# Layer norms of a recurrent kernel: eleven backward items normalised as they lie, by turned and spread mean and scale, instead of turned to tokens and back

## The chip, the cores and the metric

The kernel runs on one core of a Trainium2 chip. Its time is the device time of one execution in microseconds; runs of the same kernel are compared by their median. The engines are named as in the profile: PE (TensorE matmuls) and PEld (its weight loads), DVE (VectorE), ACT (ScalarE), POOL (GpSimd) and SP (SyncE, which here only issues DMAs). Each engine works through its own instructions in program order and waits for others by semaphores.

## The reference, cut to what matters

Input x is 8 sequences of 512 tokens with 512 features, all float32. A bidirectional recurrent stack of four layers works on the normalised x, forward and on the flipped sequence; then a linear fusion and a feed-forward part with ternary weights follow, each with a residual.

```python
def _mingru(x, Wz, bz, Wh, bh):
    z = jax.nn.sigmoid(jnp.einsum('bsi,hi->bsh', x, Wz) + bz)
    h_tilde = jnp.tanh(jnp.einsum('bsi,hi->bsh', x, Wh) + bh)
    a = jnp.clip(1.0 - z, CLAMP_LO, CLAMP_HI)
    return _linear_scan(a, z * h_tilde)          # h[t] = a[t] * h[t-1] + z[t] * h_tilde[t]

def _stack(x, Wz, bz, Wh, bh, gamma, beta):
    h = x
    for i in range(L):                           # L = 4
        h_new = _mingru(h, Wz[i], bz[i], Wh[i], bh[i])
        if i > 0:
            h_new = h_new + h
        h = _layernorm(h_new, gamma, beta)       # over the features
    return h
...
h_fwd = _stack(x, ...)
h_bwd = jnp.flip(_stack(jnp.flip(x, axis=1), ...), axis=1)
out = concat(h_fwd, h_bwd) @ fusion_W.T + fusion_b
```

Both matrices of a layer are the same weights and both directions use the same ones, so one product u per layer and item gives z, h_tilde and a. The scan runs along the tokens; the norm needs mean and variance over the features of each token.

## The kernel before

**Layout.** A state is held transposed: features on the 128 partitions in NC_ = 4 chunks, the 512 tokens along the free dimension, so that a scan is one DVE instruction per chunk. For the norm that is the wrong way round: mean and variance belong to a token, that is to a column. So `norm` turns the result: `turned` transposes the four chunks of 128 tokens into one PSUM tile `pt` (tokens on partitions, L316), `stats` takes mean and variance there (bn_stats L171, bn_aggr L173, small DVE operations L177 and L182, a power on POOL L178), `normalise` writes the normalised tokens `tok` on ACT (L188, L189), and `back` transposes them back into `pf` (L325), from where ACT writes the next layer's state with gamma and beta as per-partition scale and bias (L331).

**Items, layers, pairs.** An item is one sequence b in one direction: s = (b, 0) forward or (b, 1) backward. Sequences go in pairs (0,1), (2,3), (4,5), (6,7), called pairs 1 to 4. Layer 0 of a pair is computed in `first_layer`, interleaved with the fusion of the pair before. Layers 1 to 3 go through the items of a pair in turn, (b,0), (b,1), (b+1,0), (b+1,1), so that an item's next layer begins 16 slots after its last one did.

**Slots.** `layer` makes one `slot` for each of the 4 output chunks. A slot issues 16/4 = 4 matmuls of the gate (each two instructions in the trace, L487), the three activations a, t, z that read it (L505 to L507), the clamp of a on POOL (L511), then shares of work queued by earlier items, then on DVE the product (L514), the scan (L518) and the residual add (L588) of this gate. Two queues hold the shares: `turns` (one turn with its statistics) and `backs` (one turn back). `shares` takes the head of each queue once it is due by the slot counter `now`, and a second one only if that is late; the part that a share leaves for ACT (`last`) is issued at the slot's end. `stages` holds work due at a later slot; its kind "late" is issued right after the gate's activations. `x_shares` adds work for the next pair's x: in layers 1 and 2 of pairs 2 and 3, statistics of one tile `xn` every fourth slot. With T the first slot of an item's layer, its turns are due in slots T+5 to T+8, its backs in T+9 to T+12. `need` makes slots without a gate if an item's queued work isn't done when its next layer begins.

**Buffers.** PSUM: `ps_u` 4 (gates), `ps_t` 2 (turns), `ps_f` 2 (backs). SBUF: `z` 16, `tok` 10, states `h` 6, `t` 2 and `a` 3 per gate.

**DMA.** SP's queue is written in program order: x tiles for the next pair, the next transposed x (L105), x tiles for the fusion (`xf`, L96), in pair 4 the ternary weights and `xy`; each waits on its buffer in that order.

After the recurrent part (the first two thirds of the time) the feed-forward part follows, which the diff doesn't touch.

Of the kernel before, what the change touches and what calls it, by code (L numbers as in the profile page):

```python
# [9 lines left out]
F32 = mybir.dt.float32  # L10
F32R = mybir.dt.float32r
AF = mybir.ActivationFunctionType
ALU = mybir.AluOpType
# [3 lines left out]
P = 128  # L17
LN_EPS = 1e-5
# [6 lines left out]
def kernel(  # L25
# [26 lines left out]
    nc = tc.nc  # L52
    B, S, H = x.shape
    L = gru_wT.shape[0]
    F = fc_wT.shape[1]
    NC_ = H // P
    NT = S // P
# [7 lines left out]
    small = ctx.enter_context(tc.tile_pool(name="small", bufs=8))  # L65
    wpool = ctx.enter_context(tc.tile_pool(name="wts", bufs=1))
    hp = ctx.enter_context(tc.tile_pool(name="h", bufs=6))
    dram = ctx.enter_context(tc.tile_pool(name="x1", bufs=1, space=bass.MemoryType.DRAM))

    tokp = ctx.enter_context(tc.tile_pool(name="tok", bufs=TOK))  # L70
    xsp = ctx.enter_context(tc.tile_pool(name="xs", bufs=12))
    zp = ctx.enter_context(tc.tile_pool(name="z", bufs=ZT))
    ps_f = ctx.enter_context(tc.tile_pool(name="ps_f", bufs=2, space=PSUM))
# [34 lines left out]
    gam = const.tile([P, NC_], F32, name="gam")  # L108
    bet = const.tile([P, NC_], F32, name="bet")
# [11 lines left out]
    for i in range(2):  # L121
# [3 lines left out]
        s = fusp.tile([P, P], F32R, name=f"fpick{i}")  # L125
# [36 lines left out]
    ident = const.tile([P, P], F32, name="ident")  # L162
    make_identity(nc, ident)
    mhalf = const.tile([P, 1], F32, name="mhalf")
# [64 lines left out]
    with rec:  # L229
# [7 lines left out]
        now = [0]  # L237
        state = {}
        rsv = {}
        turns, backs = [], []  # L240

        held = [0]

        class Tokens(list):
# [4 lines left out]
            def append(self, tile_):  # L249
                super().append(tile_)  # L250
                self.at = now[0] + self.lag

        def ready(at):
            if isinstance(at, Tokens):
                return len(at) == NT and at.at <= now[0]
            return at <= now[0] and held[0] < TOK

        def shares(cap):


            last = []
            for q in (turns, backs):
                some = []
                for i in range(max(2, cap)):
                    if not q or not ready(q[0][0]):
                        break
                    at, piece = q[0][:2]
                    late = (at.at if isinstance(at, Tokens) else at) + piece <= now[0]
                    if i >= cap and not late:
                        break  # L270
                    some.append(take(q))
                last = some + last
            return last

        zlive = [0]

        left = {}

        def queue(q, key, at, piece, go):
            left[key] = left.get(key, 0) + 1  # L280
            q.append((at, piece, key, go))

        def take(q):
            _, _, key, go = q.pop(0)
            left[key] -= 1
            return go()

        def need(*keys):

            while any(left.get(k) for k in keys):  # L290
                slot(None, 2)

        def tokens(source, tok, rs, name):

            def go():
                src = source()
                found = stats(src, name, rs, tok is not None)
                if tok is None:
                    return lambda: None
                held[0] += 1  # L300

                def last():
                    tile_ = tokp.tile([P, H], F32, tag="tok", name=f"tok_{name}")
                    normalise(tile_, src, found, name)
                    tok.append(tile_)
                return last
            return go

        def turned(zs, t, name, frees=0):
            def source():  # L310
                if t == NT - 1:
                    zlive[0] -= frees
                spare = name.startswith("00_0") and t > 1
                pt = (ps_f if spare else ps_t).tile([P, H], F32, tag="pf" if spare else "pt", name=f"pt_{name}")
                for c in range(NC_):
                    nc.tensor.transpose(pt[:, ts(c, P)], zs[c][:, ts(t, P)], ident)  # L316
                return pt
            return source

        def back(toks, dst, c, affine, name):  # L320

            def go():
                pf = ps_f.tile([P, S], F32, tag="pf", name=f"pf_{name}")
                for t in range(NT):
                    nc.tensor.transpose(pf[:, ts(t, P)], toks[t][:, ts(c, P)], ident)  # L325
                if c == NC_ - 1:
                    held[0] -= NT

                def last():
                    if affine:  # L330
                        nc.scalar.activation(  # L331
                            dst()[:, c, :], pf, AF.Identity,
                            bias=bet[:, c : c + 1], scale=gam[:, c : c + 1],
                        )
                    else:
                        nc.scalar.copy(dst()[:, c, :], pf)
                return last
            return go

        def norm(s, zs, tag, pause, pair=1):  # L340

            toks, at = Tokens(), now[0] + pause

            def dst():
                if s not in state:
                    state[s] = hp.tile([P, NC_, S], F32, tag="h", name=f"h_{s[0]}{s[1]}")
                return state[s]

            for t in range(NT):
                queue(turns, s, at, t // pair, tokens(turned(zs, t, f"{tag}_{t}", NC_), toks, None, f"{tag}_{t}"))  # L350
            for c in range(NC_):
                queue(backs, s, toks, c // pair, back(toks, dst, c, True, f"{tag}_{c}"))

        def norm_last(s, tag):
            rsv[s] = small.tile([P, NT], F32, tag="rsv", name=f"rsv_{tag}")
            zs = [state[s][:, c, :] for c in range(NC_)]
            for t in range(NT):
                source, name = turned(zs, t, f"{tag}_{t}"), f"{tag}_{t}"
                queue(turns, s, now[0] + NC_ + 1, t, by_scalar(s, t, source, name) if s[0] > 1 and s[0] % 2 and s[1] == 0 else
                      tokens(source, None, rsv[s][:, t : t + 1], name))  # L360
# [17 lines left out]
        rx, scale = {}, {}  # L378
# [64 lines left out]
        def x_shares():  # L443
            return [take(q) for q in (xturns, xbacks) if q and ready(q[0][0])]
# [3 lines left out]
        stages = []  # L448
# [15 lines left out]
        def slot(work=None, cap=1, long=False):  # L464

            end = work() if work is not None else None
            due("factors")
            due("late")
            due("clamps")
            if long:  # L470
                due("scans")
            last = shares(cap) + x_shares()
            due("scans")
            if end is not None:
                end()
            due("resid")
            for f in last:
                if f is not None:
                    f()
            now[0] += 1  # L480
# [35 lines left out]
        def scan(dst, a, z, backward):  # L516
            d = slice(None, None, -1) if backward else slice(None)
            nc.vector.tensor_tensor_scan(dst[:, d], a[:, d], z[:, d], 0.0, ALU.mult, ALU.add)  # L518
# [58 lines left out]
        def layer(s, l):  # L577
            while s not in state:
                slot(None, 2)
            need(s)  # L580
            zs = []
            h = state[s]
            for o in range(NC_):
                def scans(a, z, o=o):
                    scan(z, a, z, s[1] == 1)
                    zs.append(z)
                    if l < L - 1:
                        nc.vector.tensor_tensor(z, z, h[:, o, :], ALU.add)  # L588
                    elif o == NC_ - 1:

                        for c in range(NC_):
                            def sums(c=c):
                                zlive[0] -= 1
                                nc.vector.tensor_tensor(h[:, c, :], zs[c], h[:, c, :], ALU.add)
                            stages.append((now[0] + c, "resid", sums))
                slot(gates(h, l, o, f"{s[0]}{s[1]}_{l}_{o}", scans))

                if s[0] < 2 and (l == L - 1 or o % 2) and len(extra) > 2 * NW or s == (B - 1, 1) and l == L - 1:
                    pieces(1)
            now[0] -= 1  # L600
            if l < L - 1:
                norm(s, zs, f"{s[0]}{s[1]}_{l}", 2)
            else:
                norm_last(s, f"{s[0]}{s[1]}_{l}")
            now[0] += 1
# [265 lines left out]
    for i in range(2):  # L871
# [5 lines left out]
        s = const.tile([P, P], F32R, name=f"pick{i}")  # L877
# [137 lines left out]
    for j in range(ends):  # L1015
        b, k = divmod(j, NF)
        late = []
# [22 lines left out]
        at = 12 if b == 0 else 8  # L1040
# [57 lines left out]
```

## Time and profile before

| | |
|---|---|
| time, median of 3 runs | 1712.66 us (1712.62 to 1712.66) |
| the profiled execution | 1712.95 us, of which its span 1711.2 us |
| layers 1, 2 of pair 2 | 357.90 to 427.45, 427.45 to 496.40 us |
| layers 1, 2 of pair 3 | 655.64 to 725.20, 725.20 to 794.14 us |
| layers 1, 2 of pair 4 | 953.38 to 1022.94, 1022.94 to 1091.89 us |
| granted TensorE clock | 1.00 |
| DMA | 53 GB/s over the span |

How to read it: the span runs from the first to the last instruction. A group's line gives line, engine, operation, what it writes from what, and its count, then busy time, the mean duration of one, and the idle time of the engine before it with what ended that. Durations of successive instructions of an engine overlap somewhat, so the distance from start to start is the better cost of a sequence. A matmul row that merges several instructions gives the time from the first one's start to the last one's end.

### The profile page before, as it was taken

The numbers are of one execution on the slowest core, as the hardware profiler recorded it, in microseconds if no ns is written. First come the engines' busy times: TensorE is split into PE (matmuls) and PEld (weight loads), VectorE is DVE, ScalarE is ACT, GpSimd is POOL, SyncE is SP. The second block draws the span as 40 slices with busy tenths as digits, with TensorE's granted clock in tenths as the row PEclk, the third lists the DMA queues.
The fourth block names the chain that finished last, engine by engine and source line by source line (L and its number), as shares of the span: only waits on it lengthen the run. The fifth ranks groups of instructions, "written<-read, shape, count | busy, mean of one in ns | idle before, by whom it ended". The sixth has DMA issues, their size and how long they took to land.

```text
span 1711.2 us, 19776 instructions
## 1 busy us (share of the span) xinstructions
PE 1700.3 (99%) x6440; PEld 1042.6 (61%) x6440; DVE 1389.1 (81%) x2619; ACT 1089.5 (64%) x1918; POOL 377.2 (22%) x558
## 2 busy tenths in 40 slices
PE   9999999999999999999999999999999999999999
PEld 5455554555555455555545555554688888888887
DVE  7988889889887888888788888885568768768877
ACT  5898873468886346888535688862356566666654
POOL 3333333223332222333222222321000000000000
PEclk9999999999999999999999999999999999999999
DMA  7002231150000125000012200102201101100100
GB/s 271 19 25 81 98 93 37 66 193 19 13 1 1 56 68 191 19 13 1 1 56 75 98 28 22 75 1 99 74 1 50 50 1 50 50 21 30 50 19 31
DMA packets 46599, 91.75 MB, mean 54 GB/s; under 512 B 5280, under 2 KB 5536, under 8 KB 45472
## 3 DMA queue, kind: packets, MB, share of 16 engines
q1 hardware_dynamic: 45488, 88.78, 15.1%
q10 hardware_dynamic: 1008, 1.70, 0.3%
q8 instruction: 51, 0.84, 0.2%
q14 instruction: 52, 0.43, 0.1%
HBM read 65.30 MB, written 25.17 MB: 53 GB/s over the span
## 4 chain that ended last, share of the span: by engine, by line
PE 92%; DVE 5%; ACT 2%; POOL 1%; issue 0%; DVEq 0%
PE u L487 33%; PE po L937 14%; PE ph L910 14%; PE pu L622 13%; PE u L535 6%; PE pt L316 6%; PE pf L325 4%; DVE z L518 1%; PE py L214 1%; DVE z L514 1%; DVE st L171 1%; ACT tok L189 1%; DVE z L588 1%; PE pst L948 0%; POOL rs L178 0%
## 5 line engine op out<-in xcount | busy, mean ns | idle before, releaser
L487 PE MATMUL u<-xT,gw 128*128 128x512 f32 x768 | 345.5, 593 | 0.0
L487 PE MATMUL u<-h,gw 128*128 128x512 f32 x768 | 345.5, 592 | 0.0
L518 DVE TENSOR_TENSOR_SCAN z<-a,z 128x512 f32<-128x512 f32 x224 | 277.1, 1237 | 21.8 <-DVE z L514 0.9
L511 POOL TENSOR_SCALAR a<-a 128x512 f32<-128x512 f32 x224 | 150.3, 671 | 559.2 <-ACT a L505 558.3
L487 PEld LDWEIGHTS u<-xT,gw 128*128 128x128 f32 x768 | 138.6, 190 | 138.7 <-issue 137.0
L487 PEld LDWEIGHTS u<-h,gw 128*128 128x128 f32 x768 | 138.6, 190 | 138.2 <-issue 138.2
L505 ACT ACTIVATE a<-u,ngb 128x512 f32<-128x512 f32 x192 | 131.7, 686 | 142.4 <-PE u L487 140.9
L937 PE MATMUL po<-pwq,ghi 128*128 128x512 f32 x512 | 202.8, 396 | 0.0
L171 DVE BATCH_NORM_STATS2 st<-pt 128x6 f32<-128x512 f32 x244 | 169.3, 694 | 39.2 <-PE pt L316 32.5
L937 PE MATMUL po<-pwq,glo 128*128 128x512 f32 x512 | 199.7, 390 | 0.0
L910 PE MATMUL ph<-yhi,fcq 128*128 128x512 f32 x512 | 199.7, 390 | 0.0
L910 PE MATMUL ph<-ylo,fcq 128*128 128x512 f32 x512 | 199.4, 389 | 0.0
L514 DVE TENSOR_TENSOR z<-z,t 128x512 f32<-128x512 f32 x224 | 154.8, 691 | 52.6 <-ACT z L507 52.3
L914 ACT ACTIVATE g<-ph 128x512 f32<-128x512 f32 x128 | 76.4, 597 | 186.6 <-PE ph L910 186.6
L178 POOL TENSOR_TENSOR rs<-ve,mhalf 128x1 f32<-128x1 f32 x192 | 125.5, 654 | 155.1 <-DVE nmu L182 152.7
L189 ACT ACTIVATE tok<-pt,nmr,rs 128x512 f32<-128x512 f32 x192 | 149.4, 778 | 6.4
L925 DVE TENSOR_TENSOR acc<-acc,g 128x512 f32<-128x512 f32 x112 | 77.4, 691 | 85.0 <-ACT g L914 84.1
L507 ACT ACTIVATE z<-u,gb 128x512 f32<-128x512 f32 x192 | 132.4, 690 | 0.0
L506 ACT ACTIVATE t<-u,gb 128x512 f32<-128x512 f32 x192 | 130.8, 681 | 0.0
L316 PEld LDWEIGHTS pt<-ident,z 128*128 128x128 f32 x640 | 78.7, 141 | 77.2 <-issue 48.9
L535 PE MATMUL u<-xT,gw 128*128 128x512 f32 x256 | 114.8, 593 | 0.8 <-DVE gw L767 0.8
L622 PE MATMUL pu<-fw,xT 128*128 128x512 f32 x256 | 115.2, 593 | 0.0
(164 smaller groups left out, 2621.0 us busy)
## 6 DMA issues: line engine op xcount, KB each, us to landing
xf<-in_x_dram SPq DMA_DIRECT2D x32, 256.0 KB, 5.5
x<-xf SPq DMA_DIRECT2D x32, 256.0 KB, 2.0
xy<-x SPq DMA_DIRECT2D x32, 256.0 KB, 4.0
xn<-in_x_dram SPq DMA_DIRECT2D x31, 256.0 KB, 4.5
out_dram<-xy SPq DMA_DIRECT2D x31, 256.0 KB, 2.0
xT<-in_xt_dram SPq DMA_DIRECT2D x7, 1024.0 KB, 7.7
fca<-in_fc_wT_dram SPq DMA_DIRECT2D x16, 256.0 KB, 2.9
pwa<-in_proj_wT_dram SPq DMA_DIRECT2D x16, 256.0 KB, 2.6
```

The costliest lines, as they stand in the source:

```text
L171: nc.vector.bn_stats(st, src)
L189: nc.scalar.activation(dst, src, AF.Identity, bias=nmr, scale=rs)
L316: nc.tensor.transpose(pt[:, ts(c, P)], zs[c][:, ts(t, P)], ident)
L487: nc.tensor.matmul(u, lhsT=gw[l][:, c, ts(o, P)], rhs=h[:, c, :], start=(c == 0), stop=(c == NC_ - 1),)
L507: nc.scalar.activation(z, u, AF.Sigmoid, bias=gb[:, l, o : o + 1])
L511: engine.tensor_scalar(a, a, CLAMP_HI, CLAMP_LO, ALU.min, ALU.max)
L514: nc.vector.tensor_tensor(z, z, t, ALU.mult)
L518: nc.vector.tensor_tensor_scan(dst[:, d], a[:, d], z[:, d], 0.0, ALU.mult, ALU.add)
L535: nc.tensor.matmul(u, lhsT=gw[0][:, c, ts(o, P)], rhs=xT[b][:, c, :], start=(c == 0), stop=(c == NC_ - 1),)
L622: nc.tensor.matmul(pu, lhsT=hs[d][:, c, ts(t, P)], rhs=fw[:, d * NC_ + c, :], start=(c == 0), stop=(c == NC_ - 1),)
L910: nc.tensor.matmul(ph, lhsT=w, rhs=ys[b][c][i], start=(c == 0 and i == 0), stop=(c == NC_ - 1 and i == 1),)
L937: nc.tensor.matmul(po[b][t], lhsT=part[:, ts(t, P)], rhs=pwq[k // NP_][:, k % NP_, :], start=(k == 0 and i == 0), stop=(k == NF - 1 and i ...
```

## The change

For the backward items of pairs 2 to 4, after layers 1 and 2, except sequence 7 after layer 2 (eleven norms), `norm_rows` takes the place of `norm`. The turns stay, but only to get mean and variance: of turns 0 and 1 by two ACT passes over the PSUM tile with accumulated sums, of turns 2 and 3 by bn_stats and bn_aggr on DVE. They are gathered in one tile `pk` (128 tokens x 2 x 4). Epsilon and the power -0.5 are done once for the four turns. `to_rows` then transposes `pk` on PE (8 columns), copies the 8x128 result on ACT, writes it to DRAM as two rows of 512 and reads each row back spread over all 128 partitions (`wide`). In the chunks as they lie, DVE subtracts the spread mean and multiplies by the spread scale, and ACT writes the next state with gamma and beta. Nothing is turned back, and no normalised tokens are made. The transpose is issued in slot T+9 ahead of that slot's shares, the four chunks are due in slots T+11 to T+14, ACT's write of each chunk in the slot after.

```diff
+        class Rows:
+            at = None
+
         def ready(at):
+            if isinstance(at, Rows):
+                return at.at is not None and at.at <= now[0]
...
+        LANDS = 2
+
+        def to_rows(cols, n, dsts, tag):
+            turned_ = ps_f.tile([P, S], F32, tag="pf", name=f"prow_{tag}")[0 : n * NT, 0:P]
+            nc.tensor.transpose(turned_, cols.rearrange("p i t -> p (i t)"), ident)
+            short = dsts[0][0 : n * NT, 0:P]
+            nc.scalar.copy(short, turned_)
+            row = dram.tile([n, S], F32, tag=f"row_{tag}", name=f"row_{tag}")
+            nc.sync.dma_start(out=row.rearrange("i (t p) -> (i t) p", p=P), in_=short)
+            for i, dst in enumerate(dsts):
+                nc.sync.dma_start(out=dst, in_=row[i : i + 1, :].broadcast_to([P, S]))
+
+        def norm_rows(s, zs, tag, pause, pair=1):
+            rows_, at = Rows(), now[0] + pause
+            pk = small.tile([P, 2, NT], F32, tag="pk", bufs=6, name=f"pk_{tag}")
+            wide = []
+
+            def close():
+                nc.vector.tensor_scalar(pk[:, 1, :], pk[:, 1, :], LN_EPS, None, ALU.add)
+                nc.gpsimd.tensor_tensor(pk[:, 1, :], pk[:, 1, :], mhalf.broadcast_to([P, NT]), ALU.pow)
+                stages.append((now[0] + 1, "late", send))
+
+            def send():
+                for i in range(2):
+                    wide.append(tokp.tile([P, S], F32, tag="tok", name=f"wide{i}_{tag}"))
+                to_rows(pk, 2, wide, tag)
+                rows_.at = now[0] + LANDS
+
+            def turn(t):
+                source, name = turned(zs, t, f"{tag}_{t}"), f"{tag}_{t}"
+
+                def go():
+                    src = source()
+                    if t == 0:
+                        held[0] += 2
+                    if t >= 2:
+                        st = small.tile([P, 6], F32, tag="st", name=f"st_{name}")
+                        nc.vector.bn_stats(st, src)
+                        nc.vector.bn_aggr(pk[:, :, t], st)
+                        if t == NT - 1:
+                            close()
+                        return lambda: None
+
+                    def last():
+                        sm, ss = (small.tile([P, 1], F32, tag=k, name=f"{k}_{name}") for k in ("sm", "ss"))
+                        mean, var = pk[:, 0, t : t + 1], pk[:, 1, t : t + 1]
+                        nc.scalar.activation(src, src, AF.Copy, accum_out=sm)
+                        nc.scalar.activation(mean, sm, AF.Copy, scale=1.0 / H)
+                        nc.scalar.activation(src, src, AF.Square, bias=mean, scale=-1.0, accum_out=ss)
+                        nc.scalar.activation(var, ss, AF.Copy, scale=1.0 / H)
+                    return last
+                return go
+
+            def apply(c):
+                def go():
+                    nc.vector.tensor_tensor(zs[c], zs[c], wide[0], ALU.subtract)
+                    nc.vector.tensor_tensor(zs[c], zs[c], wide[1], ALU.mult)
+                    left[s] += 1
+                    if c == NC_ - 1:
+                        held[0] -= 2
+
+                    def last():
+                        left[s] -= 1
+                        zlive[0] -= 1
+                        if s not in state:
+                            state[s] = hp.tile([P, NC_, S], F32, tag="h", name=f"h_{s[0]}{s[1]}")
+                        nc.scalar.activation(
+                            state[s][:, c, :], zs[c], AF.Identity,
+                            bias=bet[:, c : c + 1], scale=gam[:, c : c + 1],
+                        )
+                    stages.append((now[0] + 1, "late", last))
+                return go
+
+            for t in range(NT):
+                queue(turns, s, at, t // pair, turn(t))
+            for c in range(NC_):
+                queue(backs, s, rows_, c // pair, apply(c))
...
             if l < L - 1:
-                norm(s, zs, f"{s[0]}{s[1]}_{l}", 2)
+                (norm_rows if s[0] > 1 and s[1] and (s[0], l) != (B - 1, 2) else norm)(s, zs, f"{s[0]}{s[1]}_{l}", 2)
```

More of the change, by code (lines that the diff above doesn't have):

```diff
@@ L267, in shares @@
                     at, piece = q[0][:2]
-                    late = (at.at if isinstance(at, Tokens) else at) + piece <= now[0]
+                    late = (at.at if isinstance(at, (Tokens, Rows)) else at) + piece <= now[0]
                     if i >= cap and not late:
```

## The prediction

> **What bounds the kernel now.** I read the page's busy shares, its chain that ended last, and its groups:
>
> ```profile
> PE 1700.3 (99%) x6440; PEld 1042.6 (61%) x6440; DVE 1389.1 (81%) x2619; ACT 1089.5 (64%) x1918; POOL 377.2 (22%) x558
> PE 92%; DVE 5%; ACT 2%; POOL 1%; issue 0%; DVEq 0%
> L325 PE MATMUL pf<-ident,tok 128*128 128x128 f32 x768 | 112.4, 273 | 1.2 <-ACT tok L189 1.0 <-ACT h L331 0.2
> ```
>
> PE sets the end, and L325 holds the transposes back that the change takes out in part. Then the timeline of PE in layer 2 of pair 2, for one slot:
>
> ```profile
> 444.69 3.60 PE L487 MATMUL u<-h,gw 128*128 128x512 f32 x8
> 448.13 0.60 PE L316 MATMUL pt<-ident,z 128*128 128x128 f32 x4
> 448.56 0.60 PE L325 MATMUL pf<-ident,tok 128*128 128x128 f32 x4
> 449.00 3.60 PE L487 MATMUL u<-h,gw 128*128 128x512 f32 x8
> ```
>
> Starts, not durations, give the cost: gate 3.44, turn 0.43, back 0.44, slot 4.31 us. The windows by layer (layer 2 of pairs 2 and 4; columns: window, length, busy PE, PEld, DVE, ACT, POOL) tell who comes next:
>
> ```profile
> 427.45:496.40 68.95, 68.95 (x258) 37.55 (x257) 61.94 (x125) 56.05 (x98) 24.01 (x36) 1.00 0.02 8
> 1022.94:1091.89 68.95, 68.95 (x259) 37.55 (x257) 59.22 (x113) 55.59 (x98) 18.64 (x32) 1.00 0.09 31
> ```
>
> Vector is busy 90% of the layer (86% in pair 4, which takes no statistics of a next x). The timeline of DVE shows what a slot costs it:
>
> ```profile
> 453.07 0.70 DVE L171 BATCH_NORM_STATS2 st<-pt 128x6 f32<-128x512 f32 x1
> 453.81 0.18 DVE L173 BATCH_NORM_AGGREGATE mv<-st 128x2 f32<-128x6 f32 x1
> ...
> 454.15 0.68 DVE L171 BATCH_NORM_STATS2 st_x<-xn 128x6 f32<-128x512 f32 x1
> ...
> 455.16 0.68 DVE L514 TENSOR_TENSOR z<-z,t 128x512 f32<-128x512 f32 x1
> 455.94 1.23 DVE L518 TENSOR_TENSOR_SCAN z<-a,z 128x512 f32<-128x512 f32 x1
> 457.20 0.69 DVE L588 TENSOR_TENSOR z<-z,h 128x512 f32<-128x512 f32 x1
> 457.81 0.69 DVE L171 BATCH_NORM_STATS2 st<-pt 128x6 f32<-128x512 f32 x1
> ```
>
> From start to start: product 0.78, scan 1.26, residual add 0.61, together 2.65; one turn's statistics 1.08; those of x 1.01, every fourth slot.
>
> **The change on PE.** Eleven items lose 4 back groups of 4 transposes: 11 x 4 x 0.436 = 19.2 us. Each gains one transpose of 8 columns; no row has that shape, the nearest is 0.11 (a quarter of a back group), and 0.1 to 0.2 bounds it: 1.2 us. Net 18.0 us if nothing else became late. I count in units of 8 slots, one forward and one backward item: 34.47 before, 34.47 - 1.74 + 0.11 = 32.84 after. Pairs 2 and 3 have four units each, pair 4 three.
>
> **On DVE.** A unit costs 8 x 2.65 + 8 x 1.08 + 2 x 1.01 = 31.9 in pairs 2 and 3, 29.9 in pair 4. The change adds 8 tensor_tensor of 128x512 between SBUF tiles. Their rows are L588 (692 ns) and L514; the second of each two reads the first one's result as scan does product's, so 0.78 + 0.61 = 1.39 per chunk, 5.6 per item. It drops the statistics of turns 0 and 1 (2.16), four small ones of turns 2 and 3 (0.3), and adds one small (0.1). Net +3.2: 35.1 in pairs 2 and 3, 33.1 in pair 4. That is above PE's 32.84 in every unit, and above the old 34.47 in pairs 2 and 3. Vector becomes the engine that sets the pace there.
>
> **Collisions with POOL.** This is the timeline of POOL and of DVE where a clamp meets a scan in the first layers:
>
> ```profile
> 248.89 1.24 POOL L511 TENSOR_SCALAR a<-a 128x512 f32<-128x512 f32 x1
> ```
> ```profile
> 248.50 1.23 DVE L518 TENSOR_TENSOR_SCAN z<-a,z 128x512 f32<-128x512 f32 x1
> 249.65 1.03 DVE L594 TENSOR_TENSOR h<-z,h 128x512 f32<-128x512 f32 x1
> ```
>
> The clamp, 0.61 beside statistics, takes 1.24, and Vector's next operation 1.03 instead of 0.69: 0.35 us lost to DVE. Today the clamp falls beside bn_stats. After the change DVE runs over 1 us behind from the first chunk applied (5.1 us of work against a PE slot of 3.87), and in the two slots where Scalar takes the statistics there is no bn_stats at all. So clamps will meet products, scans and the new pairs. Between none and all seven lagging slots of a unit (0 to 2.45 us) I take four in pairs 2 and 3, three in pair 4, because some will fall beside bn_stats still: 1.4 and 1.05. Units: 36.5 and 34.15. The Trainium skill (GPSIMD Engine Reference, Specifications) says that GpSimd's SBUF interface is shared with VectorE and contends with DVE instructions that have two SBUF inputs; every added operation is one. By the rule alone all seven slots would count, and the sum would end near 1727.
>
> **Why the lag cannot be ridden out.** The new transpose stands in PE's queue right after the gate of slot T+9 (T: the item's first slot) and needs POOL's power of slot T+8. From the turn's end: 0.2, statistics 0.95, the added constant and its hand-over 0.3, power 1.02 (the 128x4 row rsg) and 0.1, 2.6 us, against 4.3 until PE is there: 1.4 to 1.7 of lag is allowed, then PE stands, with all later gates and turns behind it. A unit in pairs 2 and 3 has a lag near 3 at that point.
>
> **On ACT.** Out go 4 nmr and 4 tok (301 + 778 ns, 4.3 per item). In come two sets of passes, each 582 + 184 + 203 + 660 + 190 + 203 ns as in by_scalar's rows (4.0 together), and a copy of 8x128 (0.2 to 0.6 by the 128x1 and 128x512 rows; 0.25, it is small). The affine write of h stays, from SBUF: 786 to 817 ns. Even in sum, but moved: h was written in slots T+9 to T+12, now T+12 to T+15, and the next layer reads it in T+16. In T+15 the chunk stands behind three activations: ready 0.2 + 1.7 + 0.8 = 2.7 after the gate's end, plus Scalar's backlog (slots with passes hold 4.4 and 5.0 against PE's 3.9 and 4.3: 1.2). PE wants it after a turn, two backs of the forward item (which are now pushed into one slot) and three chunks: 0.44 + 0.87 + 2.57 = 3.9. Nothing is left; 0 to 2, I take 0.8 per item where DVE doesn't already set the pace.
>
> **On SP and DMA.** Three DMAs per item: rows out to DRAM and two broadcasts back. Rows: x<-xf 2.0, xy<-x 4.0, up to 5.5 (xf) and, for the one broadcast, fb at the start of the run, 8.7. Ready for DVE 2.3 + 2.0 + 4.0 + 0.5 = 8.8 after the gate of T+9; DVE gets to it at 9.6 or later (two slots of 3.9 to 4.0, the turn, 1.08). Hidden by two slots of gates; by the upper row, 4 us late per item. The Trainium skill (DMA: Bandwidth & Descriptors, Anatomy of one DMA) puts a DMA at about 2.0 us plus bytes over 436e3; as an estimate that makes 2.6 of the read, and the sum stays. SP's queue is in program order: behind the new waits stand the next pair's xT (issued at 365 now, then near 420, used at 558) and xf loads (which wait for buffers until 437 anyway); the weight loads in pair 4 wait for a layer's end anyway. POOL drops three powers of four: off the path. I take nothing for these.
>
> **Sum.** First unit of each pair: nothing applied yet, -1.6 + 0.8 = -0.8. Pairs 2 and 3: units 2 and 3, 36.5 - 34.5 = +2.0 each; unit 4 ends in layer 3, three gates there lack the residual add (1.8): +0.2. That is +3.4, twice +6.8. Pair 4: -0.8, then twice 34.15 - 34.47: -1.4. In all +5.4 on the profiled execution's 1712.95 (span 1711.2 and 1.75 around it), which is 0.29 over the median: 1718.
>
> **Rivals.** *The cover holds*: no collision, no late chunk, DVE carries some 2 us of lag out of each pair into layer 3, where slots are lighter (3.1 of 4.31 busy). Per pair -1.6 + 0.6 + 0.6 - 1.2 - 2 = -3.6; pair 4 -1.6 - 1.4 - 1.4 = -4.4: -11.6, 1701, up to 1709 with one collision per unit. For it: PE is 99% busy and sheds 18 us; against it: DVE's 35.1. *Balance*: two collisions and half the chunk's wait, gains in pair 4 pay for pairs 2 and 3: 1709 to 1716. *The rows come late*: with the 8.7 row DVE waits 2 to 4 us per item in order, with product and scan behind it; from 1 us of lateness it outweighs all else. 11 x 2.5: 1740. Against it: the queue is empty then (1 to 8 GB/s), unlike at fb.
>
> **Chances.** Forecast (1715 to 1725) 0.45; cover 0.24; balance 0.17; late rows 0.14. A measurement tells about 0.2% (3.4 us) from no change: faster 0.24, same 0.20, slower 0.56. Range 1702 to 1733: below it lies the cover's better half, above it the late rows' worse half.
>
> **What would show it.** L325 x592. DVE's busy time in layer 2 of pair 2 up from 61.9 to about 67 and its window from 68.95 to 70 or more; clamps well over 671 ns; waits of PE on POOL's power at the new transpose and of PE's loads on ACT h. Wrong if layers 1 and 2 shrink in pairs 2 and 3, if DVE waits there on a DMA, or if clamps stay at 614.

## The result, and the profile after

The changed kernel takes 1726.59 us (median of 4 runs, 1726.54 to 1726.83) against 1712.66 before (4 runs): a ratio of 1.0081, 95% interval 1.0064 to 1.0099. It is 13.9 us slower. The forecast was 1718, with a range from 1702 to 1733.

The page of the kernel after, its busy shares and the shares of its chain that ended last:

```profile
PE 1690.4 (98%) x6275; PEld 1023.9 (59%) x6275; DVE 1428.8 (83%) x2586; ACT 1086.3 (63%) x1973; POOL 394.1 (23%) x525
PE 70%; DVE 20%; ACT 6%; issue 1%; POOL 1%; DMA 1%; DVEq 0%; ACTq 0%
```

PE's part of the chain fell from 92% to 70%, and Vector's rose from 5% to 20%. The groups of the kernel after (line, engine, operation, count, then busy time and mean ns of one, then the idle time ahead of them and what ended it) show the removed and the added work:

```profile
L332 PE MATMUL pf<-ident,tok 128*128 128x128 f32 x592 | 87.0, 275 | 11.0 <-ACT xT L338 9.8 <-ACT tok L189 1.0 <-ACT h L338 0.2
L677 DVE TENSOR_TENSOR z<-z,xT 128x512 f32<-128x512 f32 x64 | 48.8, 762 | 2.2
L420 DVE TENSOR_TENSOR z<-z,wide 128x512 f32<-128x512 f32 x44 | 32.2, 731 | 0.0
L421 DVE TENSOR_TENSOR z<-z,wide 128x512 f32<-128x512 f32 x44 | 31.0, 705 | 1.5
L431 ACT ACTIVATE h<-z,bet,gam 128x512 f32<-128x512 f32 x44 | 36.1, 820 | 2.9 <-DVE z L421 2.8
```

The 176 transposes are gone (L332, formerly L325 x768), yet PE stands 11.0 us ahead of those that are left, instead of 1.2. Vector has 88 new operations with no idle time worth naming ahead of them: it comes to them late. The windows by layer (window, length, busy PE, PEld, DVE, ACT, POOL, then the granted clock, DMA share, GB/s) are layers 1 and 2 of pair 2, then layers 2 and 3 of pair 4. Those are cut from the first gate of a layer to the first gate of the next, the last one to the end of pair 4's last gate. The row below them is that last one, layer 3 of pair 4, in the kernel before:

```profile
357.69:426.04 68.35, 67.97 (x248) 36.29 (x246) 57.71 (x116) 53.65 (x99) 21.93 (x33) 1.00 0.15 48
426.04:497.93 71.89, 66.97 (x229) 33.81 (x228) 68.37 (x119) 54.46 (x105) 26.48 (x30) 1.00 0.15 51
1030.34:1099.05 68.71, 66.56 (x229) 33.97 (x228) 64.41 (x107) 55.41 (x107) 19.93 (x26) 1.00 0.13 47
1099.05:1172.19 73.14, 69.09 (x228) 35.39 (x227) 63.56 (x120) 49.15 (x84) 24.73 (x33) 0.95 0.12 44
```
```profile
1091.89:1158.59 66.70, 66.27 (x232) 34.64 (x231) 57.45 (x111) 47.07 (x82) 22.08 (x33) 1.00 0.12 48
```

Layer 2 of pair 2 went from 68.95 to 71.89 us while PE's busy time in it fell from 68.95 to 66.97 and Vector's rose from 61.94 to 68.37. Between the same events in both kernels, pairs 2 and 3 change by -1.2 in layer 1, +2.9 in layer 2 and +2.7 from layer 3 to the next pair: +4.4 each. Pair 4 changes by -1.2, by -0.2 in layer 2 and by +6.4 in layer 3 (66.70 to 73.14): +5.0. In all 13.8, against 13.6 between the two profiled spans (1711.2 and 1724.8).

A slot of Vector in layer 2 of pair 2 (its timeline: start, duration, operation), with POOL's clamp of the same slot:

```profile
468.62 0.69 DVE L171 BATCH_NORM_STATS2 st<-pt 128x6 f32<-128x512 f32 x1
...
469.69 0.68 DVE L420 TENSOR_TENSOR z<-z,wide 128x512 f32<-128x512 f32 x1
470.40 0.69 DVE L421 TENSOR_TENSOR z<-z,wide 128x512 f32<-128x512 f32 x1
471.01 0.69 DVE L603 TENSOR_TENSOR z<-z,t 128x512 f32<-128x512 f32 x1
471.80 1.23 DVE L607 TENSOR_TENSOR_SCAN z<-a,z 128x512 f32<-128x512 f32 x1
473.06 0.92 DVE L677 TENSOR_TENSOR z<-z,xT 128x512 f32<-128x512 f32 x1
473.90 0.68 DVE L420 TENSOR_TENSOR z<-z,wide 128x512 f32<-128x512 f32 x1
```
```profile
472.65 0.78 POOL L600 TENSOR_SCALAR a<-a 128x512 f32<-128x512 f32 x1 [1.88 <-ACT a L594]
```

From start to start: statistics 1.07, the two new ones 1.32, product 0.79, scan 1.26, residual add 0.84, together 5.28 us, while PE's slot with no back in it is 3.87. There is no gap in Vector's row: it is the bound in such slots. The add lasts 0.92 instead of 0.69; the clamp that starts at 472.65 runs into it, and without clamps (run 2) it is back at 0.69. Such adds are the rule: in layer 2 of pair 2, fourteen of the sixteen residual adds last 0.91 to 1.04 us.

```profile
L677 DVE TENSOR_TENSOR z<-z,xT 128x512 f32<-128x512 f32 x8 | 7.3, 916 | 0.3
```

(This is half of them, in the window of that layer alone.)

Three of PE's waits in the kernel after (total us, times, longest):

```profile
PE u L576 <- ACT h L431: 10.2, 10, 1.1
PE pf L332 <- ACT xT L338: 9.8, 7, 3.7
PE prow L366 <- POOL pk L383: 2.0, 4, 0.5
```

The new layer's gates wait for h; the backs of the forward items wait for a psum buffer that Scalar empties late (L338); the new transpose waits for POOL's power, 0.5 at most.

### The profile page after: what moved, and what is told of

It is laid out like the page before. It is cut to its first block, busy times and chain, and to the rows that moved or that the text cites. A ratio compares the mean times of both kernels' runs of the same rounds, so it can differ in the third digit from the quotient of the medians.

```text
span 1724.8 us, 19494 instructions
## 1 busy us (share of the span) xinstructions
PE 1690.4 (98%) x6275; PEld 1023.9 (59%) x6275; DVE 1428.8 (83%) x2586; ACT 1086.3 (63%) x1973; POOL 394.1 (23%) x525
## 4 chain that ended last, share of the span: by engine, by line
PE 70%; DVE 20%; ACT 6%; issue 1%; POOL 1%; DMA 1%; DVEq 0%; ACTq 0%
PE u L576 16%; PE po L1026 14%; PE ph L999 13%; PE pu L711 13%; PE u L624 6%; DVE z L607 6%; PE pt L323 4%; DVE z L603 3%; DVE z L677 3%; DVE st L171 2%; PE pf L332 2%; DVE z L421 1%; DVE z L420 1%; ACT z L596 1%; ACT a L594 1%
## 5 line engine op out<-in xcount | busy, mean ns | idle before, releaser
L576 PE MATMUL u<-h,gw 128*128 128x512 f32 x768 | 350.1, 597 | 10.2 <-ACT h L431 10.2
L600 POOL TENSOR_SCALAR a<-a 128x512 f32<-128x512 f32 x224 | 167.7, 749 | 490.8 <-ACT a L594 480.7
L171 DVE BATCH_NORM_STATS2 st<-pt 128x6 f32<-128x512 f32 x200 | 138.1, 690 | 27.9 <-PE pt L323 27.0
L178 POOL TENSOR_TENSOR rs<-ve,mhalf 128x1 f32<-128x1 f32 x148 | 106.8, 722 | 170.7 <-DVE nmu L182 168.4
L189 ACT ACTIVATE tok<-pt,nmr,rs 128x512 f32<-128x512 f32 x148 | 115.1, 777 | 4.9
```

What stands on the lines that cost most here:

```text
L171: nc.vector.bn_stats(st, src)
L576: nc.tensor.matmul(u, lhsT=gw[l][:, c, ts(o, P)], rhs=h[:, c, :], start=(c == 0), stop=(c == NC_ - 1),)
L600: engine.tensor_scalar(a, a, CLAMP_HI, CLAMP_LO, ALU.min, ALU.max)
```

## The experiments

Theory A: Vector's added operations (with their collisions with POOL's clamp) set the pace, and PE's saving has no worth. The rivals carry the letters that the expectations give them. B: the order of the new chain, with Scalar's chunks at its end. C: the two backs that the forward item now gets in one slot. D: the deadline at T+16, where the new layer reads h. E: the place of the write of h behind three activations. Each is timed beside the kernel before, on one chip.

**1. Without the two added operations.**

```diff
-                    nc.vector.tensor_tensor(zs[c], zs[c], wide[0], ALU.subtract)
-                    nc.vector.tensor_tensor(zs[c], zs[c], wide[1], ALU.mult)
```

> The changed kernel with the 88 subtracts and multiplies by the spread rows left out (the next state is then made of results that are not normalised); all transposes, passes, rows and copies back stay. Theory A (Vector sets the pace in layers 1 and 2, by its own work and by meeting POOL): Vector falls to about 29.5 us per unit of 8 slots, under PE's 32.84, and the 18 us saved on PE appear, less what is left of waits for the last chunk: 1695 to 1704. Rival B (what costs is the order of the new chain on ACT and its late chunks, not Vector's work): PE still waits for h and for the PSUM buffers of the backs, 1712 or more.

Measured: 1702.23 us, ratio 0.9939 (0.9924 to 0.9954), 10.4 us faster than before. A's 1695 to 1704 holds. All the rest of the change stands, its DMAs and its order. Nobody reads the spread rows here, but that spares Vector no wait: in the kernel after, the subtract (L420) has 0.0 us of idle time ahead of it. So these 88 operations turn a gain of 10.4 into a loss of 13.9. Page of this run, busy shares:

```profile
PE 1684.5 (99%) x6275; PEld 1023.4 (60%) x6275; DVE 1360.4 (80%) x2498; ACT 1086.2 (64%) x1973; POOL 368.2 (22%) x525
```

POOL's busy time falls with Vector's (394.1 to 368.2), though POOL has the same 525 instructions: in layers 1 and 2 of pairs 2 to 4 every residual add is back at 0.69 us, so the clamps no longer meet them.

**2. The kernel after without POOL's clamp, and 3. the kernel before without it, as a control.**

```diff
-            engine.tensor_scalar(a, a, CLAMP_HI, CLAMP_LO, ALU.min, ALU.max)
+            pass
```

> The changed kernel without the clamp of a on POOL (values stay within 1e-8 of the clamped ones). A with collisions at 0.35 us, four to seven per unit: Vector gets 1.4 to 2.4 us per unit back, and the scan no longer waits for POOL: 1706 to 1716. If the added operations alone make Vector late and collisions are small: 1722 to 1727. B: unchanged, 1724 to 1727.

> The kernel before without the clamp, as the control of the run without it: PE is the limit there and the clamp falls beside bn_stats, so 1711.5 to 1713 by every theory. Clearly less would mean that the clamp costs time in the kernel before too.

Measured: 1716.64 (ratio 1.0023, 1.0014 to 1.0033) and, for the control, 1713.3 (1.0003, 0.9994 to 1.0012). Both lie just above the ranges expected by A (1706 to 1716) and for the control (1711.5 to 1713). The clamp costs nothing that can be measured before and 10.0 us after, 0.9 per item. In run 2 the residual add is back at its 692 ns (by groups):

```profile
L677 DVE TENSOR_TENSOR z<-z,xT 128x512 f32<-128x512 f32 x64 | 44.3, 692 | 2.2
```

So the clamp makes 10.0 of the 13.9, and the rest is there without it. Most of the 10.0 is likely the collisions: from the start of the residual add to the next operation it is 0.61 us in run 2 and 0.84 in the kernel after. But run 2 also spares the scan its wait for the clamp (0.72 us from the product's start to the scan's, instead of 0.79), and doesn't tell the two apart.

**4. Two chunks applied in one slot.**

```diff
-                queue(backs, s, rows_, c // pair, apply(c))
+                queue(backs, s, rows_, c // 2, apply(c))
```

> The changed kernel with two chunks applied per slot, in T+11 and T+12, so that the last chunk of the next state is written two slots earlier; the work is the same. A: the sum on Vector is the same and comes in larger lumps: 1723 to 1730. B: the waits for h (10 us of PE in the trace of the changed kernel) go: 1714 to 1718.

Measured: 1741.04 (1.0166, 1.0151 to 1.0182), 14.5 more than the change itself and above A's 1723 to 1730. PE's waits for h are gone from the list, and that is no help (B). A missed too: in this trace the granted clock falls to half in six stretches, which no theory had in it. The last section comes back to that.

**5. The applied chunks in a queue of their own,** so that the forward item's backs aren't pushed two into a slot.

```diff
-            for q in (turns, backs):
+            for q in (turns, backs, spreads):
...
-                queue(backs, s, rows_, c // pair, apply(c))
+                queue(spreads, s, rows_, c // pair, apply(c))
```

> The changed kernel with the applied chunks in a queue of their own, so that the forward item's backs are no longer pushed together two to a slot; the work is the same. In the changed kernel's trace PE stands 12 us in all ahead of backs (for their PSUM buffer), 15 ahead of gates that read h and 3 ahead of the small transpose. A (Vector's pace, the place of the stand is a symptom): the 12 us come back at h and at the small transpose, 1722 to 1728. C (two backs in one slot with two PSUM buffers are a cost of their own): 1714 to 1718.

Measured: 1727.2 (1.0084, 1.0069 to 1.0099), the change's own time. The waits of PE only change places:

```profile
PE u L576 <- ACT h L431: 13.1, 11, 4.5
PE pf L332 <- ACT tok L189: 11.5, 12, 1.3
```

A's 1722 to 1728 holds. C falls: the crowded backs are where PE feels the lateness, not where it comes from.

**6. Ten items: sequence 6 after layer 2 by the old norm.**

```diff
-                (norm_rows if s[0] > 1 and s[1] and (s[0], l) != (B - 1, 2) else norm)(...)
+                (norm_rows if s[0] > 1 and s[1] and (s[0], l) not in ((B - 2, 2), (B - 1, 2)) else norm)(...)
```

> The changed kernel with the norm of sequence 6 backward after layer 2 as before (ten items). Layer 3 of pair 4 took 66.1 us before and 72.6 after; statistics of the first y tokens are queued at its start. If that stage is dear because the last item's chunks meet those statistics: the layer returns to 66 to 67 and the time to 1719 to 1722. If the loss is spread evenly over the eleven items (1.3 us each): 1725 to 1726.

Measured: 1722.53 (1.0058, 1.0041 to 1.0075), 4.1 less than with eleven, three times the mean of 1.3 (13.9 over 11). It lies between the two forecasts, just above the first. Windows of this run, layers 2 and 3 of pair 4, cut as above:

```profile
1030.36:1101.80 71.44, 68.02 (x240) 35.21 (x238) 67.13 (x119) 57.29 (x105) 22.77 (x29) 1.00 0.11 38
1101.80:1168.49 66.69, 66.26 (x232) 34.64 (x231) 57.60 (x112) 47.01 (x82) 22.04 (x33) 1.00 0.13 48
```

Layer 3 is that of the kernel before again (66.69 against 66.70), and the granted clock is 1.00 throughout. So the whole 6.4 us of that layer came with this item, most of whose chunks are applied there. But layer 2 takes 71.44, 2.7 more than with eleven items (68.71): the old norm keeps its backs on PE there, and it makes the item ahead of it dearer, as run 7 will show.

**7. Three items only, each the first of its pair,** with old norms behind it.

```diff
-                (norm_rows if s[0] > 1 and s[1] and (s[0], l) != (B - 1, 2) else norm)(...)
+                (norm_rows if s[0] > 1 and s[1] and s[0] % 2 == 0 and l == 1 else norm)(...)
```

> Rows only for the first backward item of pairs 2 to 4 after layer 1 (three items), all others as before. A: Vector's excess of one item (3.2 us and collisions) finds some 2.5 us of slack per unit of 8 slots in the units behind it, so that PE's saving of 1.6 us per item shows, less a wait for h: 1708 to 1711.5. B (each item costs by its late chunks wherever it stands, 1.3 us): 1715 to 1717.

Measured: 1720.64 (1.0047, 1.0032 to 1.0062): +8.0, or 2.7 per item. Both theories missed. A counted on a unit of old norms behind each item to take up the lag; it doesn't. The timeline of PE shows where the item is paid for (in brackets: how long PE stood, and for what):

```profile
441.58 0.60 PE L323 MATMUL pt<-ident,z 128*128 128x128 f32 x4
442.02 0.60 PE L332 MATMUL pf<-ident,tok 128*128 128x128 f32 x4
444.03 0.66 PE L332 MATMUL pf<-ident,tok 128*128 128x128 f32 x4 [1.42 <-ACT xT L338]
444.53 2.74 PE L576 MATMUL u<-h,gw 128*128 128x512 f32 x6
449.65 1.12 PE L576 MATMUL u<-h,gw 128*128 128x512 f32 x2 [2.38 <-ACT h L431]
```

These are slots T+15 and T+16, 6.38 and 6.95 us long; the six ahead of them took 3.87 to 4.31. PE runs six slots as fast as it is offered work, Vector falls behind, and both waits come at once when the next layer needs the last chunk of h. The lag falls due in T+15 and T+16, four and five slots after the first chunk is applied; from T+18 on the slots take 4.31 again.

The 2.7 isn't the price of an item in the full change, though. There the same two slots take 5.42 and 5.65. The old norm of the next backward item has all its statistics on Vector, two of them just ahead of the due slots, in T+13 and T+14 (timeline of Vector in this run):

```profile
437.58 0.69 DVE L171 BATCH_NORM_STATS2 st<-pt 128x6 f32<-128x512 f32 x1
...
443.87 0.69 DVE L171 BATCH_NORM_STATS2 st<-pt 128x6 f32<-128x512 f32 x1
```

In the full change Scalar takes these two. The unit behind is lighter for Vector over its eight slots, and heavier in those that count.

**8. Three turns' statistics on Scalar instead of two.**

```diff
-                    if t >= 2:
+                    if t >= 3:
```

> The changed kernel with the statistics of turn 2 by two passes on Scalar as well: Vector has 0.93 us less per item, Scalar 2.0 more. A (Vector's pace): 1717 to 1724. B (Scalar's order is what delays h and the evictions): 1727 to 1735.

Measured: 1732.24 (1.0114, 1.0099 to 1.0129). B's 1727 to 1735 holds, A's 1717 to 1724 doesn't. It takes 0.93 us off Vector in slot T+7 and puts 2.0 on Scalar there. For all but the first item of a pair that is slot T+15 of the changed item ahead, where its lag falls due; so Vector's relief is worth less there than Scalar's load costs. That Scalar's backlog is part of the 13.9 as it stands is likely by this, but not shown.

**9. The removed transposes put back on PE,** four per applied chunk, into a psum tile that nobody reads.

```diff
+                    pd = ps_f.tile([P, S], F32, tag="pf", name=f"pd_{tag}_{c}")
+                    for t in range(NT):
+                        nc.tensor.transpose(pd[:, ts(t, P)], ident, ident)
```

> The changed kernel with the removed PE work put back as idle work: four transposes of the identity ahead of every applied chunk, into a PSUM tile that nobody reads (19 us of PE in all). Theory A in its local form (Vector, in the slots where chunks are applied, is the engine that the others wait for, and PE's shorter slots there are handed back as waits a slot or two later): 1726 to 1730. If PE's saving reaches the end of the run and something else took 32 us more: 1740 to 1746.

Measured: 1727.02 (1.0083, 1.0065 to 1.0101), the change's own time, and within A's 1726 to 1730. Page of this run, PE's waits in it, and its window of layer 3 of pair 4:

```profile
PE 1703.8 (99%) x6451; PEld 1042.1 (60%) x6451; DVE 1427.2 (83%) x2586; ACT 1086.1 (63%) x1973; POOL 394.5 (23%) x525
```
```profile
PE u L579 <- ACT h L434: 5.1, 5, 1.8
PE pf L332 <- ACT xT L338: 1.8, 1, 1.8
```
```profile
1099.58:1172.01 72.43, 67.86 (x240) 35.41 (x239) 62.85 (x120) 48.70 (x84) 25.09 (x33) 1.00 0.12 44
```

PE works 13.4 us more and waits for h and for the psum buffer 13.1 us less (20.0 in the kernel after, 6.9 here). What the change takes off PE is worth nothing as long as Vector has the new operations. The clock is 1.00 throughout this run, and layer 3 of pair 4 still takes 5.7 us more than before (72.43 against 66.70; 73.14 in the kernel after, at 0.95).

**10. The write of h ahead of the slot's other activations.**

```diff
-                    stages.append((now[0] + 1, "late", last))
+                    stages.append((now[0] + 1, "first", last))
...
+            due("first")
```

> The changed kernel with ACT's write of a chunk of h issued at the head of the next slot, ahead of that slot's three activations instead of behind them. Theory D (new, after the run with three items: from slot T+9 on PE has no backs and reaches T+16 early, while the chain Vector, then ACT, then h has no slot of slack there; so Vector's lag is paid at T+15 and T+16 of each item and isn't carried to lighter units): Vector is what is late, ACT's order matters little: 1722 to 1730. E (the place behind three activations is what makes the chunk late): the 15 us that PE stands ahead of gates go, 1712 to 1716.

Measured: 1726.59 (1.0081, 1.0066 to 1.0096), the same again. The chunks of h come in time now, and the wait goes elsewhere:

```profile
PE pf L332 <- ACT xT L338: 10.9, 15, 3.0
PE prow L366 <- POOL pk L383: 8.9, 8, 1.6
PE u L577 <- ACT h L431: 1.8, 2, 0.9
```

E falls. D's range holds, but not by its mechanism alone: with h early, PE waits for the power and the backs instead. That speaks for slots that are too long for Vector and Scalar, whatever is served first.

**11. The rows spread by PE and Scalar instead of DMAs, one slot sooner, and 12. the same for the three items of run 7.**

```diff
-        LANDS = 2
+        LANDS = 1
...
-                to_rows(pk, 2, wide, tag)
+                for i in range(2):
+                    pf = ps_f.tile([P, S], F32, tag="pf", name=f"spread{i}_{tag}")
+                    for t in range(NT):
+                        nc.tensor.transpose(pf[:, ts(t, P)], pk[:, i, t : t + 1].broadcast_to([P, P]), ident)
+                    nc.scalar.copy(wide[i], pf)
```

> The changed kernel with mean and scale spread by eight transposes of a broadcast column on PE and two copies on ACT instead of one transpose and three DMAs, and the chunks due one slot earlier (T+10 to T+13). PE saves half as much (about 0.8 us per item), Vector's work is the same. D: the slot gained takes most of the 30 us that PE stands: 1714 to 1720, the rest by Vector's sum in pairs 2 and 3. A (Vector's sum alone): 1724 to 1728.

> The spreading on PE and the chunks one slot earlier for three items only (first backward item of pairs 2 to 4, after layer 1); with DMAs and a slot later this took 1720.6. D: the slot of slack lets the lag drain in the lighter slots behind: 1710 to 1713.5. If the added work on Vector costs wherever it stands: 1717 to 1721.

Measured: 1745.35 (1.0193, 1.0178 to 1.0208) and 1724.12 (1.0066, 1.0049 to 1.0083). Both lie above every forecast: a slot more until T+16 brings no gain at all. One slot sooner, three applied chunks instead of two meet the statistics of the forward item's turns on Vector. Vector's timeline of run 12 has two such statistics, one slot apart:

```profile
1032.81 0.69 DVE L171 BATCH_NORM_STATS2 st<-pt 128x6 f32<-128x512 f32 x1
...
1038.09 0.69 DVE L171 BATCH_NORM_STATS2 st<-pt 128x6 f32<-128x512 f32 x1
```

They are 5.28 us apart, the lagging slot of the kernel after. The two copies load Scalar as well, and the clock falls: five stretches at half in run 11, three in run 12. How much of the 18.8 and 3.5 us over the DMA versions is the added slot, the copies or the clock isn't told apart here.

## Why the prediction was right, and where it was not

- **PE as the bound of before and its saving of 18.0 us.** Sized rightly where it can be seen alone: layer 1, with three back groups less and one small transpose more, is 1.2 us shorter, as by these terms. But it is worth nothing in the end (run 9): the unit's 32.84 us on PE is a floor that the kernel doesn't reach.
- **Vector takes the lead; +3.2 us per unit.** Right. Its busy time in layer 2 of pair 2, two units, rose by 6.4 to 68.37 (about 67 foretold), and run 1 shows that its 88 operations make the difference of 24.4 us. The rivals of the held cover and of the balance fall with this.
- **Collisions.** Priced at four per unit in pairs 2 and 3 and three in pair 4, at 0.35 us each: the bounds sum to 6 x 1.4 + 2 x 1.05 = 10.5 us, and run 2 measures 10.0. That is near by luck, as both factors were off. In layer 2 of pairs 2 and 3 seven residual adds per unit are slowed (in pair 4 three, as taken), most of them to 0.92 us, which is 0.23 lost and not 0.35. That POOL and Vector share a way to SBUF is said by the Trainium skill (GPSIMD Engine Reference, Specifications). Here it shows as a residual add of 762 ns against 692 (run 2), and as 749 ns for a clamp instead of 671, by the rows of the kernel before and this one:

```profile
L511 POOL TENSOR_SCALAR a<-a 128x512 f32<-128x512 f32 x224 | 150.3, 671 | 559.2 <-ACT a L505 558.3
L600 POOL TENSOR_SCALAR a<-a 128x512 f32<-128x512 f32 x224 | 167.7, 749 | 490.8 <-ACT a L594 480.7
```

  So the reading of the rule by which all seven lagging slots count was right on the number of collisions in pairs 2 and 3. That its sum, near 1727, is also the measured time is chance: it stands on the price of 0.35 and on the sum by units, which failed.
- **The sum by units, and the lag carried within a unit.** This step failed. Held against the layers, the sum had -0.8 for layer 1 (first unit), +4.0 for layer 2 of pairs 2 and 3 and -0.6 in pair 4 (second and third unit), and for layer 3 +0.2 in pairs 2 and 3 (fourth unit) and nothing in pair 4. Measured are -1.2, then +2.9 and -0.2, and in layer 3 +2.7 and +6.4. So layers 1 and 2 cost 2.9 us less in all than the sum has them, and layer 3 costs 11.4 more (twice 2.5, and 6.4). Together that is the gap between 5.4 and 13.8; the forecast is as near as it is because the two partly cancel. Averaging work over 8 slots lets Vector catch up in slots without applied chunks. In fact PE runs ahead in the slots before, and the catching up is over in slots T+15 and T+16, where the next layer reads h (run 7). For the last items of a pair those slots lie in layer 3, where the sum gave them no price. The place was wrong too: the prediction had PE stand at the new transpose of T+9, behind POOL's power. There it stood 2.0 us in all, against 20.0 ahead of gates that read h and of backs without a free psum buffer.
- **Layer 3 of pair 4.** The largest miss, 6.4 us for one item (run 6). It isn't mainly the clock, which falls there for 6.83 us: run 9 has 5.7 of it at a clock of 1.00. Without the added operations on Vector (run 1) the layer is 1.9 us longer than before, so they make a difference of 4.5 there. The timeline shows why they may be dear there: Vector has statistics of the y tokens of norm_y(0) in the same slots as the chunks. No run takes these away, so that part is argued.

```profile
1111.91 0.98 DVE L421 TENSOR_TENSOR z<-z,wide 128x512 f32<-128x512 f32 x1
1112.82 0.68 DVE L171 BATCH_NORM_STATS2 st_y<-xy 128x6 f32<-128x512 f32 x1
```

- **Scalar.** "Even in sum" is right (1086.3 against 1089.5 busy), but its place matters: run 8 shows that 2.0 us more in one slot of an item cost 5.6 in all. The prediction gave it only 0.8 per item, and only where Vector didn't already set the pace.
- **DMA.** Right: hidden. The read of a row lands in 3.4 us (4.0 taken) by the list of DMA issues below, Vector doesn't wait for `wide`, and the rival of the late rows falls. The formula of the Trainium skill (DMA: Bandwidth & Descriptors, Anatomy of one DMA), which gave the prediction's estimate of 2.6, is stated there for DMAs that GpSimd issues; SP issues these.

```profile
wide<-row SPq DMA_DIRECT2D x22, 256.0 KB, 3.4
```

- **Small terms.** The transpose costs 0.11 us (0.11 taken) and the copy 0.238 (0.25). The power lasts 1.02 to 1.47, in the middle 1.32 (1.02 taken).

What stays open: how the 13.9 us divide between Vector's lateness, Scalar's backlog and the clock, and what makes layer 3 of pair 4 so dear. Runs 2, 8 and 6 give single prices (10.0, 5.6 for more of it, 4.1), but these overlap, and removing one wait moved it (runs 5 and 10).

## What to carry to other kernels

Work moved from the busiest engine to one that is 90% busy in the stage must be counted slot by slot, up to the first point where the next stage reads its result: lag isn't averaged out over the lighter slots behind that point. When removing one wait after the other leaves the time where it was (runs 5 and 10), and so does giving the waiting engine more to do (run 9), the waits are signs of a slot that is too long, and only taking work away from it moves the end (runs 1 and 2). Look also at the stage after the last changed one: here it cost more than any other.

## What the hardware showed that was not expected

PE's granted clock fell to half where PE had stood for two to four microseconds, though not each time, and the next matmuls paid again. A window of the kernel after, in layer 3 of pair 4, and the timeline of PE there:

```profile
1119.00:1123.00 4.00, 3.70 (x8) 2.16 (x9) 3.37 (x10) 3.50 (x8) 1.44 (x2) 0.50 0.00 2
```
```profile
1111.10 3.60 PE L576 MATMUL u<-xT,gw 128*128 128x512 f32 x8
...
1114.99 0.60 PE L332 MATMUL pf<-ident,tok 128*128 128x128 f32 x4
1119.30 1.12 PE L332 MATMUL pf<-ident,tok 128*128 128x128 f32 x4 [3.71 <-ACT xT L338]
1120.21 5.99 PE L576 MATMUL u<-h,gw 128*128 128x512 f32 x8
```

PE stands for 3.71 us. The clock is 0.50 (columns as in the windows above, the clock third from the end) from 1118.18, 2.6 us into the stand, for 6.83 us, and a gate of eight matmuls takes 5.99 instead of 3.60. In run 12 a shorter stand is enough:

```profile
435.07 0.49 PE L332 MATMUL pf<-ident,tok 128*128 128x128 f32 x3
438.12 0.48 PE L332 MATMUL pf<-ident,tok 128*128 128x128 f32 x1 [2.56 <-ACT tok L189]
438.39 4.91 PE L580 MATMUL u<-xT,gw 128*128 128x512 f32 x8
```

The clock is 0.50 from 437.61 for 3.41 us, and so it is once for each of the three items, after stands of 2.1 to 2.6 us. In the 3.41 us ahead of these falls PE otherwise had transposes, and gates for 1.0 us at most. In the profiled execution of run 7 a stand of 2.38 us amid gates brought no fall; two of its other executions have a mean clock of 0.999 and are 1.2 us or more longer, so a fall in those isn't excluded. Neither the kernel before nor runs 1, 6, 7 and 9 have such a stretch in their profiles, short of the run's very end. The Trainium skill (TensorE: Matmul & The Clock Gate, Why this matters for your kernels) says "No PE-idle gaps >~3µs between matmul bursts". The 3.71 agrees with that and the 2.1 to 2.6 don't; its Part 4 adds that a transpose doesn't count as busy PE in the same way, which would fit the stands of run 12, though no run here changes the transposes alone. So a wait that looks like 2 us can cost more, and that is a price which a trace without the wait doesn't show.

The other surprise is how much a POOL operation of 0.6 to 0.8 us can cost elsewhere: leaving it out brings 10.0 us where Vector is late (run 2) and nothing where it isn't (run 3).
